# A two-layer graph kernel on one core: another order of head, step and tail, the first graph's x first on the DMA queue, fillers of other lengths

## The chip, the core and the metric

The kernel runs on one core of a Trainium2 chip. A core has five engines with a queue each: TensorE (PE, matrix products), VectorE (DVE), ScalarE (ACT), GpSimd (POOL) and SyncE (SP), which here only issues transfers. Each queue is worked off in order. An instruction that waits for another engine holds up everything behind it on its own engine. The metric is the device time of one execution in microseconds, as the median of several runs. The kernel before takes 2449.39 us (3 runs, 2448.46 to 2452.33).

## What is computed

For each of 128 graphs of 128 nodes with 512 features, in fp32:

```python
h = relu(layernorm(x))
H = (adj != 0);  w = adj[0, :]            # per graph
conv(v, W, b) = Dinv * (H @ (Binv * (H.T @ (v @ W.T)))) + b
t = relu(conv(h, W1, b1))                 # 512 -> 1024
y = conv(layernorm(t) * gamma + beta, W2, b2) + h   # 1024 -> 512
x = x + y
h = relu(layernorm(x))
agg = (adj @ h) / max(rowsum(adj), EPS)
x = x + relu(concat(h, agg) @ W.T)        # 1024 -> 512
```

`Dinv` and `Binv` are inverse weighted degrees of nodes and of hyperedges.

## The kernel before, in words

One graph is one tile: 128 nodes on the partitions, the features along the row. The weights stay in SBUF. Every large product is made with fp32 accuracy out of fp32r matrix products: each operand is split into a high part, a low part and a correction (suffixes h, l, d). `product` (L517 to L537) then issues the h and l passes into one PSUM bank (L530) and the d pass into a second (L535). Six banks carry the tag `w`, two the tag `n`. ACT makes the high part (a copy with a scale), DVE or POOL the low part, DVE the third.

A graph goes through these stages, each a small function marked `@stage`:

- `incidence...`, `node_matrix`, `node_sum`: adj is loaded in a blocked layout, transposed on DVE (L390), compared with zero (L393), its edge count and its weight scaled; PE makes the graph's 128x128 operator into `ps_s` (L430), ACT (L432) and DVE (L438) move it to SBUF as `s`.
- `x_sums`, `x_spread`, `scales`, `shifts`, `x_norm`: layer norm of x on ACT, with two tiny operations on DVE, POOL or ACT.
- `conv1_nodes` (PE, `pz`, L488), `conv1_high/low/rest` (split on ACT L501, DVE L505, L508), `conv1_weights` for two halves (PE, `rm` and `rd`), `conv1_main` (ACT L550), `conv1_out` (DVE L555), `conv1_bias` (POOL).
- `inner_...`: layer norm over 1024, then a transpose by a trip through DRAM: `inner_out` writes the tile, `inner_in` reads it in blocks by four transfers, `inner_turn` turns the blocks on DVE (L591, `nt`).
- `conv2_weights` (PE, `gm`, `gd`), `conv2_main` (ACT L690), `conv2_weights_out` (DVE L694), `conv2_bias` (POOL), `conv2_high/low/rest` and `node_high/rest` (splits), `conv2_nodes` (PE, `ym`, `yd`; at the ends of the kernel, one unsplit product `py`, L738), `conv2_out` (DVE L754).
- `layer1_...`: the layer norm of the new x, a trip through DRAM like the first (`h_scratch`, `hb`, turned into `ht`), `layer1_mean` (PE, `bm`, `bd`), `layer1_self` (PE, `am`, `ad`), `aggregate` (PE, L832), `finish` (DVE L844) and `store`.
- `mean_...`: adj divided by its row sum, turned by a third trip through DRAM (`an_scratch`, `anb`).

The order of the work is written out by hand. `head()` starts the first graphs and prepares the weights; `step(s)` for s from 3 to 124 (122 times) is the pipeline, in which the stages of seven graphs, s-4 to s+3, are interleaved; `tail()` lets the last five run out. Within a manual schedule the order of the calls is the order of each engine's queue. So a line moved in `step` moves all instructions of that stage on every engine that it uses, its transfers on SP included.

`fill(columns)` puts idle matrix products of a constant in front of the next bank's user (L100), so that PE has something to do. Tiles mostly have one buffer: `r`, `adj`, `adjb`, `ht` and the three split tiles among them. A stage that writes such a tile waits until the graph before has been read out of it.

`copy` is an ACT activation. The trace of the kernel before has one load of an activation table, 1.28 us long, and it stands ahead of `copy(eps_root, eps, AF.Sqrt)` in `head`, the first activation.

Of the kernel before, what the change touches and what calls it, by code (L numbers as in the profile page):

```python
# [24 lines left out]
def gnn_kernel(  # L25
# [760 lines left out]
    @stage  # L786
    def layer1_low(g, *eng):
        H3T[g][0](*eng)
# [67 lines left out]
    def step(s):  # L856
        node_high(s - 2)
        conv2_bias(s - 2)
        conv2_high(s - 2)
        layer1_self_main(s - 4)  # L860
        layer1_high(s - 3)
        inner_out(s - 1)
        conv2_low(s - 2, nc.vector)
        x_norm(s + 1)
        node_rest(s - 2)
        conv1_main(s, 0)
        layer1_self_out(s - 4)
        conv2_rest(s - 2)
        node_matrix(s + 1)
        conv1_weights(s, 1)  # L870
        conv1_out(s, 0)
        mean_out(s - 3)
        layer1_low(s - 3)
        layer1_rest(s - 3)
        inner_in(s - 1)
        conv2_nodes(s - 2)
        node_sum(s + 1)
        node_floor(s + 1, nc.gpsimd)
        conv2_out(s - 2)
        conv1_main(s, 1)  # L880
        conv1_out(s, 1)
        inner_turn(s - 1)
        layer1_sums(s - 2)
        mean_in(s - 3)
        layer1_spread(s - 2)
        conv1_bias(s, 0)
        load_adj(s - 2)
        incidence(s + 2)
        layer1_mean(s - 3)
        incidence_weight(s + 2, nc.vector)  # L890
        scales(s - 2, 3)
        layer1_mean_main(s - 3)
        finish(s - 4)
        conv1_bias(s, 1)
        shifts(s - 2, 3, nc.vector)
        conv1_nodes(s + 1)
        store(s - 4)
        load_x(s + 2)
        inner_high(s - 1)
        conv1_high(s + 1)  # L900
        mean_transpose(s - 3)
        layer1_mean_out(s - 3)
        layer1_self(s - 3)
        mean_operator(s - 2)
        inner_low(s - 1, nc.vector)
        inner_rest(s - 1)
        layer1_norm(s - 2)
        inner_sums(s)
        layer1_mean_high(s - 3)
        inner_spread(s)  # L910
        conv2_weights(s - 1)
        layer1_mean_low(s - 3, nc.vector)
        node_scale(s + 1)
        mean_rest(s - 3)
        layer1_trip_out(s - 2)
        x_sums(s + 2)
        incidence_count(s + 2, nc.vector)
        mean_degree(s - 2, nc.vector)
        conv2_main(s - 1)
        scales(s, 2)  # L920
        layer1_mean_rest(s - 3)
        layer1_trip_in(s - 2)
        conv1_low(s + 1)
        incidence_inverse(s + 2)
        residual(s + 1)
        mean_inverse(s - 2)
        conv2_weights_out(s - 1)
        conv1_rest(s + 1)
        shifts(s, 2, nc.gpsimd)
        load_adjb(s + 3)  # L930
        inner_norm(s)
        incidence_high(s + 2)
        layer1_turn(s - 2)
        x_spread(s + 2)
        aggregate(s - 3)
        mean_scale(s - 2, nc.vector)
        incidence_scale(s + 2, 0, nc.vector)
        scales(s + 2, 1)
        conv1_weights(s + 1, 0)
        incidence_scale(s + 2, 1, nc.vector)  # L940
        shifts(s + 2, 1, nc.vector)
        residual_bias(s + 1)
        node_up(s + 1, nc.vector)

    def head():
        load_w1(0, 0)
        load_adjb(0, nc.scalar)
        load_x(1)
        incidence(0)
        copy(eps_root, eps, AF.Sqrt)  # L950
        load_affine()
        load_x(0)
        incidence_weight(0, nc.gpsimd)
        incidence_count(0, nc.vector)
        load_w1(0, 1)
        incidence_inverse(0)
        x_sums(1, "A")
        x_sums(0)
        w1[0].high(0)
        w1[0].high(1)  # L960
        load_x(2)
        load_w1(1, 0)
        w1[0].low(0)
        incidence_high(0)
        x_spread(0)
        scales(0, 1)
        incidence_scale(0, 0, nc.gpsimd)
        incidence_scale(0, 1, nc.scalar)
        load_w1(1, 1)
        w1[0].low(1)  # L970
        w1[0].rest(1, nc.vector)
        load_adjb(1)
        shifts(0, 1, nc.gpsimd)
        x_norm(0)
        node_matrix(0)
        fill(768)
        w1[1].high(1)
        load_w2(0)
        node_sum(0)
        incidence(1)  # L980
        conv1_nodes(0)
        w1[1].high(0)
        residual(0)
        node_floor(0, nc.vector)
        incidence_count(1, nc.vector)
        load_adjb(2)
        w1[0].rest(0, nc.vector)
        x_spread(1)
        load_bias(b2_bc, b2)
        load_bias(b1_bc, b1)  # L990
        w1[1].low(1)
        incidence_inverse(1)
        conv1_high(0)
        conv1_low(0)
        conv1_rest(0)
        node_scale(0)
        incidence_weight(1, nc.gpsimd)
        conv1_weights(0, 0)
        incidence_high(1)
        w1[1].low(0)  # L1000
        incidence_scale(1, 0, nc.scalar)
        w1[1].rest(0, nc.vector)
        incidence_scale(1, 1, nc.scalar)
        load_adj(0)
        node_up(0, nc.scalar)
        conv1_main(0, 0)
        scales(1, 1)
        load_w2(1)
        node_matrix(1)
        shifts(1, 1, nc.gpsimd)  # L1010
        incidence(2)
        node_sum(1)
        incidence_count(2, nc.gpsimd)
        beta_row(0)
        conv1_out(0, 0)
        w1[1].rest(1, nc.vector)
        x_sums(2)
        beta_row(1)
        conv1_weights(0, 1)
        incidence_weight(2, nc.vector)  # L1020
        node_floor(1, nc.gpsimd)
        x_spread(2)
        scale_w2(0, nc.vector)
        scales(2, 1)
        x_norm(1)
        beta_row(2)
        load_x(3)
        shifts(2, 1, nc.gpsimd)
        incidence_inverse(2)
        conv1_bias(0, 0, nc.vector)  # L1030
        scale_w2(1, nc.scalar)
        w2[0].high(0)
        beta_row(3)
        incidence_high(2)
        conv1_nodes(1)
        load_adjb(3)
        scale_w2(2, nc.vector)
        conv1_main(0, 1)
        load_w3(1)
        mean_operator(0)  # L1040
        node_scale(1)
        scale_w2(3, nc.scalar)
        incidence_scale(2, 0, nc.vector)
        incidence_scale(2, 1, nc.scalar)
        w2[0].high(1)
        conv1_out(0, 1)
        residual_bias(0)
        conv1_high(1, True)
        node_matrix(2)
        conv1_bias(0, 1, nc.vector)  # L1050
        beta_row(4)
        beta_row(5)
        x_norm(2)
        node_sum(2)
        conv1_nodes(2)
        mean_degree(0, nc.vector)
        node_up(1, nc.gpsimd)
        node_floor(2, nc.vector)
        inner_sums(0)
        inner_spread(0)  # L1060
        residual(1)
        node_scale(2)
        residual(2)
        load_adjb(4)
        conv1_low(1)
        scale_w2(5, nc.vector)
# [3 lines left out]
        incidence_weight(3, nc.gpsimd)  # L1070
        conv1_rest(1)
        incidence_count(3, nc.gpsimd)
        scales(0, 2)
        incidence_inverse(3)
        conv1_low(2)
        beta_row(6)
        shifts(0, 2, nc.vector)
        beta_row(7)
        w2[1].high(0)
        conv1_rest(2)  # L1080
        incidence_high(3)
        w2[0].low(1)
        unit()
        scale_w2(6, nc.vector)
        inner_norm(0)
        x_sums(3)
        scale_w2(7, nc.scalar)
        w2[0].low(0)
        mean_inverse(0)
        w2[1].low(0)  # L1090
        node_up(2, nc.scalar)
        incidence_scale(3, 0, nc.vector)
        w2[1].high(1)
        conv1_weights(1, 0)
        conv1_weights(1, 1)
        incidence_scale(3, 1, nc.scalar)
        conv1_main(1, 0)
        conv1_main(1, 1)
        inner_out(0)
        w2[0].rest(0)  # L1100
        inner_in(0)
        conv1_out(1, 0)
        x_spread(3)
        w2[0].rest(1)
        conv1_out(1, 1)
        conv1_bias(1, 0, nc.vector)
        conv1_bias(1, 1, nc.vector)
        inner_sums(1)
        node_matrix(3)
        conv1_weights(2, 0)  # L1110
        scales(3, 1)
        incidence(4)
        w2[1].low(1)
        inner_spread(1)
        w2[1].rest(1, nc.gpsimd)
        incidence_weight(4, nc.vector)
        load_x(5)
        inner_turn(0)
        beta_out()
        scales(1, 2)  # L1120
        conv1_weights(2, 1)
        incidence_count(4, nc.gpsimd)
        inner_high(0)
        shifts(1, 2, nc.scalar)
        node_sum(3)
        inner_norm(1)
        w3[1].high(1)
        w3[1].high(0)
        load_x(4)
        shifts(3, 1, nc.gpsimd)  # L1130
        inner_low(0, nc.vector)
        load_w3(0)
        incidence_inverse(4)
        inner_rest(0)
        x_norm(3)
        w2[1].rest(0, nc.vector)
        incidence_high(4)
        conv2_weights(0)
        mean_scale(0, nc.scalar)
        conv1_nodes(3)  # L1140
        conv2_main(0)
# [419 lines left out]
```

## Time and profile before

| What | us |
|---|---|
| median of 3 runs | 2449.39 |
| the profiled execution | 2447.67 |
| its span, first to last instruction | 2445.9 |
| PE busy in the span | 2422.7 |
| DVE busy | 2298.1 |
| ACT busy | 2009.9 |
| POOL busy | 1324.8 |
| PE idle from 0 to 16.88, before its first product with weights | 12.34 |
| PE idle from 16.88 to 71 | 2.55 |
| PE idle from 71 to 2353 | 0.35 |
| PE idle from 2353 to the last matmul's end at 2440.73 | 2.78 |
| from there to the end | 5.17 |

The page gives busy times of each engine and its share of the span; waits are listed as "engine, line, what was waited for: total, times, longest". In the timeline each row is a start, a duration, an engine and a line. Rows that follow each other are merged ("x4"). Matmul ends are modelled, so neighbouring rows overlap; the distance between two starts is the safer measure of what an instruction costs its queue. The same holds on DVE and ACT, where the next start comes some 0.06 to 0.1 us before the printed end of the one before. The granted TensorE clock is 1.00 in every slice. The step recurs every 18.74 to 18.75 us: the product `gm` starts at 1203.46, 1222.20 and 1240.95.

### The profile page before, as it was taken

Reading aid. Unit: us, or ns where it says so; the run is one execution under the profiler, and the core shown is the slowest. Engines: PE = TensorE matmul, PEld = TensorE weight load, DVE = VectorE, ACT = ScalarE, POOL = GpSimd, SP = SyncE. Lnnn points to the kernel's source line nnn. Section 1 sums busy time; section 2 is a strip of 40 time slices with the busy share of each in tenths; the row PEclk is TensorE's granted clock in tenths of the full one; section 3 lists DMA queues with packets and bytes.
Section 4 is the critical chain, followed back from the end, with each engine's and each line's share of the span. In section 5 each row is a group of like instructions: output and inputs, shape, how many; then the busy total and the mean of one; then the engine's idle time right before and its main releaser. Section 6 shows DMA issues by size and latency. Waiting matters only on the chain.

```text
span 2445.9 us, 41647 instructions
## 1 busy us (share of the span) xinstructions
PE 2422.7 (99%) x11170; PEld 2009.6 (82%) x11170; DVE 2298.1 (94%) x5843; ACT 2009.9 (82%) x4512; POOL 1324.8 (54%) x1808
## 2 busy tenths in 40 slices
PE   7999999999999999999999999999999999999998
PEld 5788888888888888888888888888888888888886
DVE  8899999999999999999999999999999999999987
ACT  8888888888888888888888888888888888888785
POOL 5555555555555555555555555555555555555552
PEclk9999999999999999999999999999999999999999
DMA  6344433344434443444344443434343444344432
GB/s 186 114 129 125 130 124 129 124 130 128 129 119 130 132 126 123 129 129 127 124 128 128 126 129 123 132 123 130 122 133 121 130 127 131 119 131 131 127 124 92
DMA packets 408956, 311.39 MB, mean 127 GB/s; under 512 B 176656, under 2 KB 339984, under 8 KB 408720
## 3 DMA queue, kind: packets, MB, share of 16 engines
q1 hardware_dynamic: 407888, 308.66, 40.1%
q8 instruction: 88, 1.44, 0.2%
q14 instruction: 148, 1.21, 0.2%
q10 hardware_dynamic: 576, 0.07, 0.0%
q0 software_dynamic: 256, 0.01, 0.0%
HBM read 166.21 MB, written 142.34 MB: 126 GB/s over the span
## 4 chain that ended last, share of the span: by engine, by line
PE 95%; ACT 2%; DVE 1%; DMA 1%; issue 1%; SPq 0%; POOL 0%; POOLq 0%; DVEq 0%; ACTq 0%
PE gm L530 19%; PE rm L530 18%; PE am L530 9%; PE bm L530 9%; PE gd L535 9%; PE rd L535 9%; PE bd L535 5%; PE ad L535 5%; PE pz L488 4%; PE am L832 2%; PE ad L832 1%; PE ym L743 1%; PE yd L744 1%; PE ym L742 1%; PE ps_s L430 1%
## 5 line engine op out<-in xcount | busy, mean ns | idle before, releaser
L306 ACT ACTIVATE h<-x_t 128x512 f32<-128x512 f32 x255 | 159.1, 624 | 291.8 <-DVE x_t L754 283.8
L81 POOL TENSOR_TENSOR r<-r,b_bc 128x256 f32<-128x256 f32 x500 | 358.7, 739 | 70.1 <-DVE r L555 54.4
L300 POOL TENSOR_SCALAR st<-st 128x1 f32<-128x1 f32 x130 | 82.3, 633 | 569.9 <-DVE st L317 563.2
L81 POOL TENSOR_TENSOR hl<-ht,hh 128x256 fp32r<-128x256 f32 x250 | 235.4, 963 | 216.5 <-ACT hh L612 216.5
L81 POOL TENSOR_TENSOR x_t<-x_t,h 128x256 f32<-128x256 f32 x256 | 239.8, 959 | 1.3 <-ACT h L326 1.1
L81 POOL TENSOR_TENSOR g<-g,c 128x256 f32<-128x256 f32 x246 | 177.6, 743 | 72.4 <-DVE g L694 72.4
L326 ACT ACTIVATE h<-x_t,st 128x512 f32<-128x512 f32 x255 | 206.1, 808 | 2.0 <-POOL st L300 1.2
L555 DVE SCALAR_TENSOR_TENSOR r<-rd,dinv,r 128x512 f32<-128x512 f32 x256 | 190.8, 746 | 7.7 <-ACT r L550 6.3
L81 POOL TENSOR_TENSOR x_t<-x_t,b_bc 128x256 f32<-128x256 f32 x256 | 187.2, 752 | 0.0
L311 ACT ACTIVATE h<-x_t,st 128x512 f32<-128x512 f32 x255 | 182.9, 717 | 4.1
L550 ACT ACTIVATE r<-rm,dinv 128x512 f32<-128x512 f32 x256 | 174.7, 684 | 7.7 <-PE rm L530 4.4
L694 DVE SCALAR_TENSOR_TENSOR g<-gd,g 128x512 f32<-128x512 f32 x127 | 87.8, 691 | 79.5 <-issue 70.4
L621 DVE SCALAR_TENSOR_TENSOR nd<-nh,nl 128x1024 fp32r<-128x1024 f32 x127 | 155.5, 1225 | 4.2
L326 ACT ACTIVATE r<-r,st 128x1024 f32<-128x1024 f32 x128 | 157.8, 1233 | 0.1
L591 DVE STREAM_TRANSPOSE nt<-nb 128x1024 f32<-128x1024 f32 x127 | 156.9, 1235 | 0.4 <-DMA nb<-n_scratch 0.3
L81 DVE TENSOR_TENSOR nl<-nt,nh 128x1024 fp32r<-128x1024 f32 x127 | 153.5, 1208 | 1.9 <-ACT nh L612 1.7
L530 PE MATMUL am<-w31h,hh 128*128 128x512 f32 x504 | 146.8, 413 | 0.0
L311 ACT ACTIVATE junk<-r,st 128x1024 bf16<-128x1024 f32 x128 | 145.2, 1134 | 0.1
L488 PEld LDWEIGHTS pz<-s,h 128*128 128x128 f32 x1024 | 134.5, 192 | 11.1 <-ACT h L326 0.7
L530 PE MATMUL rm<-w11h,z 128*128 128x512 f32 x512 | 140.3, 396 | 0.0
L530 PE MATMUL rm<-w11l,z 128*128 128x512 f32 x512 | 139.3, 393 | 0.0
L530 PE MATMUL rm<-w10h,z 128*128 128x512 f32 x512 | 138.2, 392 | 0.9 <-ACT z L501 0.9
(244 smaller groups left out, 7594.1 us busy)
## 6 DMA issues: line engine op xcount, KB each, us to landing
n_scratch<-r SPq DMA_DIRECT2D x128, 512.0 KB, 2.6
nb<-n_scratch SPq DMA_DIRECT2D x508, 128.0 KB, 2.8
x_t<-in_x_dram SPq DMA_DIRECT2D x128, 256.0 KB, 2.7
h_scratch<-h SPq DMA_DIRECT2D x127, 256.0 KB, 2.3
hb<-h_scratch SPq DMA_DIRECT2D x508, 64.0 KB, 1.9
out_dram<-o SPq DMA_DIRECT2D x127, 256.0 KB, 2.0
adj_t<-in_adj_dram SPq DMA_DIRECT2D x128, 64.0 KB, 1.9
an_scratch<-adj_t SPq DMA_DIRECT2D x128, 64.0 KB, 1.6
```

The lines of the kernel that those rows point to most:

```text
L81: eng.tensor_tensor(dst[:, s], a[:, s], b[:, s], op)
L306: copy(junk, src, func, accum_out=t[:, 0:1])
L311: copy(junk, src, AF.Square, bias=t[:, 1:2], accum_out=t[:, 2:3])
L326: copy(dst, src, func, bias=t[:, 5:6], scale=t[:, 4:5])
L488: nc.tensor.matmul(z[:, k * P : (k + 1) * P], H0[g][:, k * P : (k + 1) * P], S[g], start=True, stop=True)
L530: nc.tensor.matmul(pm, left[i](k), right(i, k), start=(i == 0 and k == 0), stop=(i == 1 and k == kk - 1))
L535: nc.tensor.matmul(pd, left[2](k), right(2, k), start=(k == 0), stop=(k == kk - 1), skip_group_check=True)
L550: copy(R[g][:, HALVES[half]], PY.pop((g, half)), AF.Copy, scale=DN[g][:, 1:2])
L555: nc.vector.scalar_tensor_tensor(r, PR.pop((g, half)), dn[:, 0:1], r, MUL, ADD)
L591: nc.vector.transpose(nt.rearrange("p k (i b) -> p k i b", b=B), t.rearrange("p i k a -> p k i a"))
L621: nc.vector.scalar_tensor_tensor(t, h, 2.0**-12, low, MUL, SUB)
L694: nc.vector.scalar_tensor_tensor(G[g], PG.pop(g), 4096.0, G[g], MUL, ADD)
```

## The change

The set of stages stays. What changes is the order of the calls in `head`, `step` and `tail`, the engine of some tiny operations, and the fillers: 768 columns in front of the first `pz` become 1152, and 256 columns in front of the second `pz` are new. In `step`, the weight of the incidence goes from DVE to ACT. In `head`, x of graph 0 is the first transfer on SP, ahead of the first weights; a copy of weights (`w1[0].high(0)`) stands ahead of the square root of eps on ACT; x of graph 2 is issued behind the second graph's adj. No new function is called. The core of the diff:

```diff
     def step(s):
+        conv2_bias(s - 2)
+        layer1_self_main(s - 4)
+        conv1_weights(s, 1)
         node_high(s - 2)
-        conv2_bias(s - 2)
         conv2_high(s - 2)
-        layer1_self_main(s - 4)
+        mean_out(s - 3)
+        node_rest(s - 2)
         layer1_high(s - 3)
         inner_out(s - 1)
+        conv1_main(s, 0)
         conv2_low(s - 2, nc.vector)
+        layer1_low(s - 3)
+        layer1_self_out(s - 4)
+        conv1_out(s, 0)
+        node_matrix(s + 1)
+        conv2_rest(s - 2)
+        layer1_rest(s - 3)
         x_norm(s + 1)
...
+        conv1_main(s, 1)
+        conv2_nodes(s - 2)
+        layer1_mean(s - 3)
+        node_sum(s + 1)
         inner_in(s - 1)
...
+        conv2_out(s - 2)
...
+        layer1_sums(s - 2)
         conv1_out(s, 1)
+        conv1_bias(s, 0)
+        layer1_self(s - 3)
         inner_turn(s - 1)
...
+        incidence(s + 2)
+        layer1_mean_main(s - 3)
+        incidence_count(s + 2, nc.vector)
+        load_adj(s - 2)
         mean_in(s - 3)
...
-        incidence_weight(s + 2, nc.vector)
+        incidence_weight(s + 2, nc.scalar)
         scales(s - 2, 3)
-        layer1_mean_main(s - 3)
+        conv1_nodes(s + 1)
         finish(s - 4)
...
+        inner_high(s - 1)
+        inner_sums(s)
         shifts(s - 2, 3, nc.vector)
...
         store(s - 4)
+        layer1_norm(s - 2)
+        mean_transpose(s - 3)
         load_x(s + 2)
-        inner_high(s - 1)
+        inner_low(s - 1, nc.vector)
+        layer1_mean_out(s - 3)
+        layer1_mean_high(s - 3)
+        inner_rest(s - 1)
...
+        conv2_weights(s - 1)
+        load_adjb(s + 3)
+        layer1_mean_low(s - 3, nc.vector)
         conv1_high(s + 1)
...
     def head():
+        load_adjb(0, nc.scalar)
+        load_x(0)
         load_w1(0, 0)
-        load_adjb(0, nc.scalar)
+        w1[0].high(0)
         load_x(1)
         incidence(0)
+        load_w1(0, 1)
         copy(eps_root, eps, AF.Sqrt)
         load_affine()
-        load_x(0)
-        incidence_weight(0, nc.gpsimd)
-        incidence_count(0, nc.vector)
-        load_w1(0, 1)
+        x_sums(0)
...
         incidence_inverse(0)
+        w1[0].low(0)
+        x_spread(0)
         x_sums(1, "A")
-        x_sums(0)
-        w1[0].high(0)
+        incidence_high(0)
+        scales(0, 1)
         w1[0].high(1)
+        load_adjb(1)
         load_x(2)
...
         incidence_scale(0, 1, nc.scalar)
...
+        node_matrix(0)
+        w1[1].high(1)
         w1[0].low(1)
+        incidence(1)
+        fill(1152)
...
-        node_matrix(0)
-        fill(768)
...
+        conv1_main(0, 1)
+        fill(256)
+        load_bias(b2_bc, b2)
+        conv1_out(0, 1)
+        mean_operator(0)
         conv1_nodes(1)
...
     def tail():
...
+        conv2_weights_out(d)
...
+        layer1_turn(c)
+        conv2_bias(d, nc.vector)
+        mean_scale(d, nc.vector)
+        layer1_high(c)
...
-        conv2_weights_out(d)
-        conv2_bias(d, nc.vector)
-        layer1_turn(c)
-        mean_scale(d, nc.gpsimd)
...
```

The order of the built program on each engine, which shows how the change moves instructions, has one row on ACT that the text of the change does not show. Where the kernel before loads an activation table once, ahead of the square root, the changed kernel loads one ahead of `w1[0].high(0)` and another ahead of the square root:

```
1 L274 DMACopy adjb<-in_adj_dram 32x4x32 x4
2 L179 LoadActFuncSet
3 L179 Activation w10h<-w10r 128x1024
4 L953 LoadActFuncSet
5 L953 Activation eps_root<-eps 128x1
6 L306 Activation h_125,st<-x_t 128x512
```

## The prediction

> **What bounds the kernel now.** I read the page's head first, then the waits of PE, then the busy times of PE in stretches, and last the timeline of one step and of the first 20 us.
>
> ```profile
> span 2445.9 us, 41647 instructions
> PE 2422.7 (99%) x11170; PEld 2009.6 (82%) x11170; DVE 2298.1 (94%) x5843; ACT 2009.9 (82%) x4512; POOL 1324.8 (54%) x1808
> ```
>
> PE is idle for 23.2 us of the span. Its waits say where (columns: engine, line, what was waited for, total, times, longest):
>
> ```profile
> PE ps_s L430 <- ACT sb L298: 11.4, 1, 11.4
> PE py L738 <- DVE g L81: 2.1, 2, 1.1
> PE py L738 <- POOL w11ds L81: 1.7, 1, 1.7
> ```
>
> Each happens once or twice: head and tail. In stretches PE is idle 12.34 us up to 16.88, 2.55 us from there to 71, 0.35 us from 71 to 2353, 2.78 us to the last matmul and 5.17 us behind it. So the 122 steps run on PE alone, 18.74 us each. They cannot get shorter by a new order: the list of matmuls per step is the same, and a new order can only open gaps. What can be won is 2.55 + 0.35 + 2.78 = 5.7 us, plus whatever brings the first product forward. How near DVE and ACT are to the limit, from their waits between 500 and 2300 us, 96 steps:
>
> ```profile
> DVE g L694 <- issue: 57.6, 96, 0.6
> ```
>
> ```profile
> ACT h L306 <- DVE x_t L754: 230.9, 96, 2.7
> ```
>
> DVE has one gap per step, 0.6 us, ahead of L694, where it waits for `gd` on PE. ACT has a gap of 2.4 us ahead of `layer1_sums`.
>
> **The step.** I walk each queue in the new order by hand. Zero is the start of the first `rm` of `conv1_weights(s, 1)`, 1212.25 in the timeline; intervals are distances between starts in that step. PE in the new order: rm 0, rd 1.82, ps_s 2.73, ym 2.85, yd 3.33, bm 3.55, bd 5.37, am 6.28, ad 8.10, pz 9.01, gm 9.81, gd 13.52, aggregate 15.33, rm of the next half 16.01, end 18.74. ps_s moves behind `rm`, pz behind `am`; each position of gm and gd is within 0.1 us of before.
>
> DVE is fixed to PE at two points. At 15.59 L694 may start (before: aggregate's start plus 0.26). Near 3.40 L438 may start: ps_s ends at 2.85, ACT copies it (0.27, start some 0.2 later). That second wait is new. Behind it on ACT stand `x_norm` and the second `conv1_main`, which go from about 0.5 and 2.05 to 3.3 and 4.0. It costs nothing: x_norm is needed by pz at 9.01, the bank of `rm` by am at 6.28, and ACT's gap of 2.4 us was there anyway. From L694 to L438 DVE has 0.61 + 0.59 + 0.26 + 0.63 + 0.08 + 0.19 + 0.13 + 0.18 + 0.08 + 0.21 + 0.20 + 0.61 + 0.60 + 0.68 + 0.68 + 0.61 = 6.34 us of work in a room of 3.40 + 18.74 - 15.59 = 6.55. From L438 to L694 it has 11.7 us and a wait of 0.1 for ACT's L312, in a room of 12.19. The sum is what it was, less 0.07 for the weight that went to ACT. So DVE keeps 0.2 + 0.4 = 0.6 us.
>
> PE's needs: gp's correction L731 is ready at 2.6, yd wants it at 3.33. hd ends at 3.3 for bd at 5.37. On ACT, L801 starts at 7.3, the added L298 (0.15 to 0.2 us) follows, `nh` runs 7.95 to 9.0 for gm at 9.81 (before 8.7 for 9.79). nl ends at 10.3 for 11.7, nd at 12.1 for 13.5, bl and bd at 13.1 and 14.4 for 15.5, the split of z at 12.2, 15.1 and, a round later, 16.9 for 16.0, 16.9 and 17.8. All in time: cost 0.
>
> SP: four `adjb` issues of 0.46 us now stand ahead of `h_scratch`, and on ACT L306/L307 of `inner_sums` (1.18 us) ahead of the `layer1_norm` that feeds it. `layer1_norm` ends at 11.0 (before 10.1); store at 8.7, x at 9.1 and adjb at 9.55 to 11.4 let `h_scratch` go at 11.45 (before 10.12). It lands 2.3 later, four `hb` issues take 1.3 to the last one, which lands 1.9 later: 17.0. DVE comes to `ht` at 17.05 (before: 15.85 for 16.94). The cover shrinks from 1.1 us to 0.05, with DVE's 0.6 behind it. `n_scratch` goes at 16.15 (before 16.4), behind hb and `an_scratch`; the four nb land at about 5.2 for `nt` at 5.7, as before. `adj_t` and `anb` follow and land by 7.5, for 8.5 and 8.8.
>
> A rule speaks against this: the Trainium skill, SBUF — State Buffer (SBUF: two separate sides), says that a DVE operation with two SBUF inputs and a POOL operation that reads SBUF take one port pair in turn, each for a whole instruction. The trace agrees in one place per step:
>
> ```profile
> 1219.43 1.90 POOL L81 TENSOR_TENSOR x_t<-x_t,h 128x256 f32<-128x256 f32 x2
> ...
> 1219.68 1.04 DVE L844 SCALAR_TENSOR_TENSOR o<-o,x_t 128x512 f32<-128x512 f32 x1
> ```
>
> L844 takes 0.65 in the tail and 1.04 here. In the new order POOL's `hl` meets gp and L731, and its x_t meets nl. By bare durations that is 0; by the rule 0.2 + 0.15. I take 0 for PE, since both ends stay below DVE's 0.6.
>
> **The head.** ACT loads a second table, between `w10h(0)` and eps_root. The row:
>
> ```profile
> 2.69 1.28 ACT L950 ACT_TABLE_LOAD   x1 [2.69 <-issue]
> 3.99 0.20 ACT L950 ACTIVATE eps_root<-eps 128x1 f32<-128x1 f32 x1
> ...
> 10.85 0.40 ACT L298 ACTIVATE sb<-adjt,sb 128x128 fp32r<-128x128 f32 x1
> ```
>
> The new first load lies under the transfers. Then `w10h(0)` waits for 256 + 512 KB; before, that many bytes (first weights, then x of graph 1) had landed at 5.74. So 5.75 + 1.04, table 1.28, eps 0.2: x_sums(0) starts at 8.2 (before 6.60); x landing first buys nothing, as ACT comes to it late. Then 0.86 + 1.04 + 0.86 + 0.1 + 0.95 + 0.55 to ps_s(0): 12.6 (before 11.40), +1.2. By the page ScalarE: Activation LUTs (What ACT_TABLE_LOAD costs) a switch takes 2.66 us, with a drain of 1.38. The row shows 1.28 and eps_root 0.02 behind it, but on an engine that had nothing to drain. I take the row; the page would add 1.4.
>
> The filler of 768 columns took from 11.75 to 14.31, 3.33 ns each; 1152 take 3.84 and end at about 16.8. x_norm(0) is ready at 12.05 + 0.35 + 1.04 + 0.95 + 0.25 + 0.95 + 0.81 = 16.4, so the filler costs 0.4 and the rest is ACT's order. pz starts at 16.8, +2.5 against 14.31; it takes 1.63 slow or 0.85 fast (51.62 shows the fast one), and `rm` follows by 16.88's distance: 18.6 to 19.4 against 16.88. Say +2.2. The filler of 256 columns adds 0.43 us at the fast rate, or 0 if PE waits for s there anyway. Back come some of the head's 2.55 us: `rm` of graph 3 now stands between gd(1) and the `wd` products, which saves waits of 0.39 and 0.2; but `conv1_out(2,0)` (0.66) goes ahead of `conv2_bias(0)`, for which py waits. DMA: x of graph 2 goes from 4.6 to about 10.5; ACT wants it near 20. Sum +2.2 + 0.3 - 0.5 = +2. Ends: 0, if later waits soak up the late start, and +4 with the drain and cold products.
>
> **The tail.** PE's last five rounds have the same order but for pz and ps_s. py still stands behind the bias of graphs d and e. `layer1_turn(c)` (0.7) goes ahead of `conv2_bias(d)`: py +0.7, the bm behind it -0.65. Sum 0, ends -2 (most of the 2.78) and +2.
>
> **The sum.** Execution 2447.67 + 0 (steps) + 2 (head) + 0 (tail) = 2449.7. The median stood 1.7 above this execution: 2451.4.
>
> **The rivals.** (1) The h trip and DVE become the loop of the step, slower. If hb lands later than about 17.6 (0.6 behind my 17.0), or port waits add up to more than DVE's 0.6, the excess is paid in each step: 0.1 us is 12.2 us. For it: cover of 0.05 at ht, DVE at 97%, hb landings up to 3.0 in the trace. Against: medians of 1.9, and two cushions. A likely excess of 0.05 to 0.2 gives 2457 to 2476. (2) Head and tail get better: the start is soaked up and half of the tail's waits go: 2446 to 2448; more than 4.9 below would need nearly all of the 5.7 us and no late start. (3) The change does nothing: same steps, and the head's late start absorbed: 2449.4; it lies inside the first range.
>
> **How the numbers follow.** Likeliest case with (3), 2447.5 to 2454.5: 0.60. Rival (1): 0.32. Rival (2): 0.08. 0.2% is 4.9 us, about what a measurement can tell from no change. Faster by more: 0.04 out of (2). Slower: all but a little of (1), and the top of the first case: 0.33. Same: 0.63. The range runs from 2447 to 2472: it leaves out half of (2) and the upper third of (1).
>
> **What would show it.** Right: PE idle from 71 to 2353 under 2 us, gm every 18.74, ps_s(0) near 12.6, pz(0) near 16.8, two table loads. Wrong: a wait of `bm`, `yd` or `nh` repeated 122 times (rival 1), DVE waiting for hb, the first `rm` at or before 17, or a PE step other than 18.74.

## The result and the profile after

The changed kernel takes 2463.27 us (median of 5, 2461.16 to 2463.65) against 2449.39 (5 runs, 2448.46 to 2452.33): ratio 1.0052, 95% interval 1.0038 to 1.0067, so 13.9 us slower. The profiled execution took 2463.27, its span 2461.5.

The head of the page, first the span, then the busy times. PE has the same products as before but for the fillers, DVE is 3.9 us less busy, ACT 18.5 us more:

```profile
span 2461.5 us, 41531 instructions
...
PE 2427.9 (99%) x11174; PEld 2007.9 (82%) x11174; DVE 2294.2 (93%) x5732; ACT 2028.4 (82%) x4632; POOL 1306.7 (53%) x1797
```

PE's waits (total, times, longest). The first line is the head, 0.7 us more than before. The next two are new, and they lie in the steps: `yd` waits for its operands, but in 16 of 118 steps, not in each. (The releaser is inferred. `yd` does not read the `h` of L326; in all 16 it starts 0.15 us behind the end of L731.)

```profile
PE ps_s L430 <- ACT sb L298: 12.1, 1, 12.1
PE yd L744 <- DVE sp L731: 4.7, 10, 0.9
PE yd L744 <- ACT h L326: 3.6, 6, 0.6
PE py L738 <- DVE g L81: 2.8, 2, 1.5
PE py L738 <- POOL w11ds L81: 1.7, 1, 1.7
PE pz L488 <- ACT h L326: 1.2, 1, 1.2
```

DVE's waits between 500 and 2300 us. Before, its one large wait was L694, 57.6 us in 96 steps. That has shrunk to 15.2, and a wait for hb, here as it was before, leads the list:

```profile
DVE ht L591 <- DMA hb<-h_scratch: 0.5, 1, 0.5
```

After:

```profile
DVE ht L591 <- DMA hb<-h_scratch: 20.1, 29, 1.5
...
DVE g L694 <- issue: 15.2, 54, 0.3
DVE s L438 <- ACT s L432: 8.6, 35, 0.3
DVE ht L591 <- PE rm L530: 5.1, 5, 1.1
```

The five waits put down to `rm` are for hb too: ht starts 0.12 or 0.18 us behind hb's landing in them, as in the others. ACT's gap ahead of `layer1_sums` (230.9 us before) is split in two, as ps_s now comes later:

```profile
ACT s L432 <- PE ps_s L430: 180.8, 96, 2.2
ACT h L306 <- DVE x_t L754: 82.6, 95, 1.9
```

To place the loss I cut each profiled execution at three marks on PE: the first `rm`, the first and the last `yd` of the steps. "Long" are the intervals from yd to yd over 18.95 us; a usual interval is 18.75, and the sum is what the long ones exceed the usual one by. The marks are of one execution each, and the executions of the kernel before alone lie between 2446.82 and 2453.05 us, so a difference of 1 or 2 us between two rows is weak.

```
                  median   first rm  first yd  yd..yd    last yd..last matmul  long: n, sum
before            2449.39  16.88     108.58    2194.92   137.23                 5,  1.5
after             2463.27  18.38     109.53    2208.20   138.24                21, 12.3
step_alone        2461.05  16.68     108.57    2208.32   136.96                20, 12.1
head_alone        2453.86  18.45     110.04    2198.45   137.60                11,  4.2
tail_alone        2450.98  16.56     108.33    2194.79   139.74                 2,  0.8
adjb_back         2553.75  18.86     110.69    2298.47   137.68               115, 105.1
h_first           2543.12  18.63     110.73    2289.18   137.51               117,  95.8
adjb_early        2457.60  18.69     109.55    2202.04   138.18                13,  6.5
early_norm        2460.51  17.89     109.73    2205.61   138.54                18, 10.3
turn_late         2453.26  18.78     109.77    2197.25   137.08                 4,  1.8
adjb_between      2452.31  17.81     109.55    2199.04   138.58                 9,  4.3
before_adjb       2475.95  17.09     108.88    2223.79   136.98                41, 30.0
mended            2449.73  16.73     107.73    2199.36   136.56                 8,  3.7
mended_old_ends   2448.78  16.49     109.89    2195.52   137.48                 1,  0.7
```

Of the changed kernel's 15.2 us between the two last matmuls (2440.73 and 2455.97), 0.95 is in the head, 13.3 in the steps and 1.0 in the tail. Against usual steps the loss there is 14.8 us, and it was 1.5 before: 12.3 lie in 21 long steps, 2.5 in 32 that are 0.03 to 0.2 us longer, mostly those behind a long one, in which DVE, now nearly without gaps, works off its delay. (The two waits of yd listed sum to 8.3 us, not to 13.3: the 16 intervals are 0.69 us longer in the mean, with a listed wait of 0.52, and the waits in the other five long ones are too short to be listed.)

**One late step.** Rows of SP's queue in one step and, behind the dots, in the next:

```profile
1191.21 1.88 SPq L274 DMA_DIRECT2D adjb<-in_adj_dram  x4
1193.19 0.38 SPq L576 DMA_DIRECT2D h_scratch<-h  x1
1195.26 1.73 SPq L584 DMA_DIRECT2D hb<-h_scratch  x4
...
1211.94 0.38 SPq L576 DMA_DIRECT2D h_scratch<-h  x1
1215.52 1.73 SPq L584 DMA_DIRECT2D hb<-h_scratch  x4
```

From `h_scratch` to `hb` SP waits for the landing: 2.07 us in the first step, 3.58 in the second. What this does to DVE and, a step boundary later, to PE:

```profile
1218.87 0.71 DVE L591 STREAM_TRANSPOSE ht<-hb 128x512 f32<-128x512 f32 x1 [1.16 <-DMA hb<-h_scratch]
```

```profile
1223.19 0.47 PE L744 MATMUL yd<-sp 128*128 128x512 f32 x1 [0.52 <-DVE sp L731]
```

ht is 1.16 us late. DVE's own 0.6 takes up half, and L731, the eleventh operation behind ht, is 0.52 late for yd. It is the same in all 16: DVE takes 4.18 us from the start of ht to the end of L731, which is the median of the other steps too, and yd starts 4.32 to 4.33 us behind ht. So nothing between ht and yd is slower, and the delay comes in with hb. The DMA view of the late trip, 1211.9 to 1215.5, shows what else was moved; in the step before, 1193.1 to 1195.3, there was only q1, which carries the kernel's own transfers:

```profile
q8 instruction: 1, 0.02, 2.5%
q14 instruction: 1, 0.01, 0.6%
...
h_scratch<-h SPq DMA_DIRECT2D x1, 256.0 KB, 3.5
```

q8, of the kind "instruction", carries 89 packets in the execution, 1.46 MB, so 16.4 KB each. I counted them for every step between the issue of x and ht: all 16 steps in which yd waits have one; of the 102 others, 15 have one. With them the trip is late at one of three places: the landing of h_scratch (3.1 to 3.6 us instead of 2.1, in 6 of the 16), the landing of hb (6), or SP's own issues (4; four adjb took 3.39 us instead of 1.88 at 1021). The kernel before has them too: in seven of its steps hb was issued 3.3 to 3.5 us behind h_scratch instead of 2.5, each with a q8 packet, and yd never waited.

### The profile page after: what moved, and what is told of

Same layout as the page of the kernel before. It is cut to its first block, busy times and chain, and to the rows that moved or that the text cites. A ratio compares the mean times of both kernels' runs of the same rounds, so it can differ in the third digit from the quotient of the medians.

```text
span 2461.5 us, 41531 instructions
## 1 busy us (share of the span) xinstructions
PE 2427.9 (99%) x11174; PEld 2007.9 (82%) x11174; DVE 2294.2 (93%) x5732; ACT 2028.4 (82%) x4632; POOL 1306.7 (53%) x1797
## 3 DMA queue, kind: packets, MB, share of 16 engines
q8 instruction: 89, 1.46, 0.3%
## 4 chain that ended last, share of the span: by engine, by line
PE 86%; ACT 5%; DVE 4%; DMA 2%; issue 1%; SPq 1%; POOL 0%; DVEq 0%; ACTq 0%
PE rm L530 17%; PE gm L530 16%; PE bm L530 8%; PE am L530 8%; PE rd L535 8%; PE gd L535 8%; PE pz L488 4%; PE bd L535 4%; PE ad L535 4%; PE am L832 2%; PE yd L744 1%; DMA hb<-h_scratch 1%; PE ad L832 1%; PE ym L743 1%; PE ym L742 1%
## 5 line engine op out<-in xcount | busy, mean ns | idle before, releaser
L81 POOL TENSOR_TENSOR hl<-ht,hh 128x256 fp32r<-128x256 f32 x242 | 216.5, 914 | 169.0 <-ACT hh L612 169.0
L432 ACT ACTIVATE s<-ps_s 128x129 f32<-128x129 f32 x128 | 35.8, 279 | 227.5 <-PE ps_s L430 227.5
L326 ACT ACTIVATE h<-x_t,st 128x512 f32<-128x512 f32 x255 | 205.0, 804 | 2.0 <-DVE st L300 2.0
L555 DVE SCALAR_TENSOR_TENSOR r<-rd,dinv,r 128x512 f32<-128x512 f32 x256 | 189.7, 741 | 2.6 <-ACT r L550 1.9
L550 ACT ACTIVATE r<-rm,dinv 128x512 f32<-128x512 f32 x256 | 173.8, 680 | 16.1 <-DMA n_scratch<-r 10.9
L326 ACT ACTIVATE r<-r,st 128x1024 f32<-128x1024 f32 x128 | 157.9, 1234 | 0.8 <-DVE st L300 0.8
L530 PE MATMUL gm<-w20h,nh 128*128 128x512 f32 x508 | 147.7, 412 | 0.0
L530 PE MATMUL bm<-w30h,hh 128*128 128x512 f32 x504 | 138.0, 396 | 0.0
```

The source lines that it names most:

```text
L81: eng.tensor_tensor(dst[:, s], a[:, s], b[:, s], op)
L326: copy(dst, src, func, bias=t[:, 5:6], scale=t[:, 4:5])
L530: nc.tensor.matmul(pm, left[i](k), right(i, k), start=(i == 0 and k == 0), stop=(i == 1 and k == kk - 1))
L550: copy(R[g][:, HALVES[half]], PY.pop((g, half)), AF.Copy, scale=DN[g][:, 1:2])
L555: nc.vector.scalar_tensor_tensor(r, PR.pop((g, half)), dn[:, 0:1], r, MUL, ADD)
```

## The experiments

Theory: the cover of the h trip (the time by which hb lands ahead of its use) is gone, so DVE waits for hb in the steps in which the trip is late, and yd stands behind it. Rivals: the new place of ps_s and x_norm, or a shared port, delays yd; or head and tail carry the loss. Each run below has its own comparison with the kernel before (2448.59, 2449.70 and 2449.42 us in the three groups).

**step_alone**: head and tail of before, `step` of after.

> The kernel before with the new step alone; head and tail as before. Theory (the h trip comes late in some steps, DVE waits for hb, and yd behind it): the steps carry nearly all of the loss, 2449.4 + 13.3 = 2462.7 us, with a wait of yd for L731 or L326 in about 16 of 118 steps. Rival (head and tail carry it: second table load, the first product 1.5 us later): within 1 us of 2449.4.

2461.05 us, ratio 1.0048 (1.0035 to 1.0060): +12.5, and 13.4 us more from yd to yd, with 18 waits of yd. The loss is in the step. (19 of its 20 long steps have a q8 packet.)

**head_alone**: `head` of after, the rest of before.

> The kernel before with the new head alone. Theory: the head carries 1 us of the loss (yd of the first steady step comes at 109.5 where it came at 108.6): 2450.4 us, first rm near 18.4, no wait of yd in the steps. Rival (head and tail): +5 us or more.

2453.86 us, ratio 1.0020 (1.0013 to 1.0027): +5.3, which neither side had. Only 1.5 us of it lie ahead of the first yd. 3.5 lie in the steps, whose order is that of before: 11 long ones instead of 5. PE's waits for it are short, and they are for DVE:

```profile
PE ps_s L430 <- DVE st L300: 0.7, 3, 0.4
```

The parts are not additive (12.5 + 5.3 + 1.3 is more than 13.9): with the new step, the new head adds nothing between the yd marks (2208.20 and 2208.32).

**adjb_back**: undo one move of the change.

```diff
-        load_adjb(s + 3)          # ahead of layer1_mean_low(s - 3)
...
         conv1_rest(s + 1)
+        load_adjb(s + 3)
```

> The changed kernel with load_adjb(s + 3) moved back behind conv1_rest(s + 1), so that h_scratch no longer stands behind four adjb issues on SP. Theory: h_scratch goes when layer1_norm ends, 11.05 us after the first rm instead of 11.48; each stall of yd shrinks by up to 0.43, and those below that vanish: some 5 us of 13 stay, 2455.5 us (2453 to 2458). Rival (ps_s and x_norm behind the first rm, or a shared port, set the stalls): 2463, unchanged.

2553.75 us, ratio 1.0432 (1.0418 to 1.0447). Both sides missed by 90 us and more. ACT's waits between 500 and 2300 us name what I had overlooked:

```profile
ACT r L550 <- DMA n_scratch<-r: 122.9, 86, 2.3
```

Behind adjb on SP stands `n_scratch`. It now goes 18.65 us after the first rm of `conv1_weights(s, 1)` in the median (16.31 in the changed kernel), and the tile r that it reads has one buffer. `conv1_main(s, 0)`, which the change moved near the front of the step, writes that tile. So the early conv1_main needs an early n_scratch, and moving adjb away from there was part of the same bargain; adjb_between, below, tests this.

**h_first**: as adjb_back, and `inner_sums(s)` moved behind `layer1_norm(s - 2)`.

> The changed kernel with load_adjb(s + 3) moved back behind conv1_rest(s + 1) and inner_sums(s) moved behind layer1_norm(s - 2): SP and ACT both let h_scratch go first. Theory: h_scratch goes about 9.8 us after the first rm (11.48 in the changed kernel, 10.12 before), hb lands 1.7 us earlier, ahead of nearly every ht; 0 to 1.6 us of the 13.3 stay, and head and tail keep their 2: 2450 to 2453 us. Rival (ps_s and x_norm behind the first rm, or a shared port): 2463, unchanged.

2543.12 us, ratio 1.0380 (1.0365 to 1.0394): the same wall, L550 waits for n_scratch 80.1 us in 56 steps. So it does not test the h trip.

**adjb_early**: adjb where SP was idle.

```diff
         mean_in(s - 3)
+        load_adjb(s + 3)
...
-        load_adjb(s + 3)
```

> The changed kernel with load_adjb(s + 3) moved forward behind mean_in(s - 3), into SP's idle stretch ahead of the store, instead of ahead of h_scratch. Putting it behind hb cost 90 us, because n_scratch then went 1.9 us later and r, which has one buffer, waited for it. Here nothing is put between hb and n_scratch. Theory (h trip late, cover 0.05): h_scratch goes 11.05 us after the first rm instead of 11.48 and is never held by adjb; of the 13.3 us lost in the steps some 4 stay: 2454 us (2451 to 2457), with at most 6 waits of yd. Rival (ps_s and x_norm behind the first rm, or a shared port): 2463, unchanged.

2457.60 us, ratio 1.0032 (1.0020 to 1.0043): about half of the step's loss is back, on the theory's side but above its upper bound by a little. adjb, with one buffer, waits for L393 and pushes store and x up to h_scratch. h_scratch goes at 10.93 (11.48 in the changed kernel), but SP goes on to hb 2.29 us later in the median instead of 2.09, and over 3 us later in 23 steps instead of 7.

**early_norm**: adjb_early, and `inner_sums(s)` behind `layer1_norm(s - 2)`.

> The changed kernel with load_adjb(s + 3) moved forward behind mean_in(s - 3) and inner_sums(s) moved behind layer1_norm(s - 2). Theory: h_scratch goes about 9.9 us after the first rm (before: 10.12), the cover of hb is 1.1 us or more again, and nearly all of the 13.3 us come back; head and tail keep some 2: 2450 to 2452 us. If the later inner_sums makes n_scratch late, ACT's L550 waits for it and the time is above that of adjb_early. Rival (ps_s and x_norm behind the first rm, or a shared port): 2463.

2460.51 us, ratio 1.0045 (1.0032 to 1.0057): a miss. h_scratch goes at 10.00, as I wanted, but its trip takes 3.30 in the median, and over 3 us in all but one of the steps. It went 1.48 us earlier than in the changed kernel and was there 0.27 earlier. The load of x, 256 KB issued 0.53 us before it, is still on the way. It is so in the other runs too (x lands 2.7 to 3.1 us behind its issue); what differs is the distance. Medians, in us; "its trip" is the time until SP issues hb:

```
               h_scratch behind x   its trip   sum
early_norm     0.53                 3.30       3.83
h_first        0.77                 3.17       3.94
before         1.24                 2.52       3.76
adjb_early     1.46                 2.28       3.72
adjb_between   1.90                 2.04       3.95
after          2.46                 2.09       4.55
```

Up to a distance of 1.9 the sum stays between 3.72 and 3.95: an issue closer to that of x did not bring hb's issue forward. That x's bytes hold the store up would fit; no run takes x away.

**turn_late**: the transfers stay, the one who waits for them comes later.

```diff
-        layer1_turn(s - 2)        # behind x_spread(s + 2)
...
         node_up(s + 1, nc.vector)
+        layer1_turn(s - 2)
```

> The changed kernel with layer1_turn(s - 2) alone moved, to the end of the step behind node_up(s + 1): five short DVE operations, 0.63 us, go ahead of ht. SP and ACT keep their order and the transfers go when they did. Theory: the cover of hb grows from 0.05 to 0.7; what is left of the single stalls (0.3 to 0.9 us each) is about 2 us, so 2452 us (2451 to 2455), and DVE's waits for hb fall from 29 to a few. Rival (the cost is a shared port or the place of ps_s, and hb only shows it): 2463.

2453.26 us, ratio 1.0015 (1.0008 to 1.0021): 10 of the 13.9 us are back with no transfer moved. PE's waits in the steps, all of them:

```profile
PE yd L744 <- DVE sp L731: 1.0, 2, 0.8
```

Between 500 and 2300 us DVE's waits for hb are gone from its list; one wait of 1.1 us at ht is left. The edit leaves the place of ps_s and of x_norm as it is, so these do not cause the stalls. It does move five DVE operations against POOL's; that no port is behind it rests on the 4.18 us above, which are the same in stalled and other steps.

**tail_alone**: `tail` of after, the rest of before.

> The kernel before with the new tail alone. By the distance from the last yd of the steps to the last matmul (137.23 us before, 138.24 in the changed kernel) the tail costs 1 us: 2449.6 against 2448.6. If the losses of head and steps overlap and the tail gives something back, it is 1 to 3 us below the kernel before.

2450.98 us, ratio 1.0007 (1.0001 to 1.0014): +1.3. The tail costs 1 to 2.5 us by the marks (138.24 and 139.74 against 137.23).

**adjb_between**: adjb goes while SP waits for n_scratch anyway.

```diff
         inner_out(s - 1)
+        if s > 3:
+            load_adjb(s + 2)
...
-        load_adjb(s + 3)
+        if s == N - 4:
+            load_adjb(s + 3)
```

> The changed kernel with the adjb of the next graph issued between n_scratch and nb, that is load_adjb(s + 2) behind inner_out(s - 1), and not ahead of h_scratch. Putting it between hb and n_scratch cost 90 us. If that cost was n_scratch going 1.9 us later, with L550 waiting for the one buffer of r, it vanishes here, since SP waits 2.6 us for n_scratch to land at this point anyway: L550's waits for n_scratch fall from 123 us to under 10, and with h_scratch at 11.05 the time is that of adjb_early or a little less, 2455 us (2452 to 2458). If the cost was something else about taking adjb away from ahead of h_scratch, it stays above 2500.

2452.31 us, ratio 1.0014 (1.0007 to 1.0020). h_scratch goes at 10.93, its trip takes 2.04, n_scratch goes at 16.06, and ACT's wait between 500 and 2300 us is:

```profile
ACT r L550 <- DMA n_scratch<-r: 6.0, 17, 0.9
```

So the 90 us of adjb_back were n_scratch, and hb's landing 0.7 us earlier saves two thirds of the step's loss (13.3 to 4.1).

**before_adjb**: one move of the change in the kernel before.

```diff
+        load_adjb(s + 3)
         layer1_trip_out(s - 2)
...
-        load_adjb(s + 3)          # behind shifts(s, 2)
```

> The kernel before with one edit of the change alone: load_adjb(s + 3) ahead of layer1_trip_out(s - 2). SP then issues four adjb between x and h_scratch, which goes at about 11.2 us after the first rm instead of 10.12; hb lands 1.1 us later, and its cover of 1.1 is gone. Theory: this edit is most of the loss, 2449 + 8 to 13 = 2457 to 2462 us, with DVE waiting for hb in the steps in which an instruction packet delays the trip. Rival (the cover alone costs little; it takes the new order of DVE, ACT and PE as well): 2449 to 2452.

2475.95 us, ratio 1.0106 (1.0092 to 1.0120): +26.5, twice what I expected and twice the whole change. h_scratch goes at 11.37. The wait on PE is another:

```profile
PE ps_s L430 <- DVE st L300: 19.8, 32, 1.6
```

The rows of one such step, DVE, then PE:

```profile
1243.76 0.71 DVE L591 STREAM_TRANSPOSE ht<-hb 128x512 f32<-128x512 f32 x1 [0.78 <-DMA hb<-h_scratch]
1244.40 0.25 DVE L300 TENSOR_SCALAR adj_t<-adj_t,deg 128x128 f32<-128x128 f32 x1
1244.56 0.28 DVE L300 TENSOR_SCALAR sb<-adjt,sb 128x128 fp32r<-128x128 f32 x1
1244.83 0.27 DVE L300 TENSOR_SCALAR sb<-adjt,sb 128x128 fp32r<-128x128 f32 x1
...
1245.25 0.36 PE L430 MATMUL ps_s<-sb,adjt 128*128 128x258 f32 x1 [0.49 <-DVE st L300]
```

In the old order ps_s stands ahead of `rm`, and the sb that it needs comes one operation behind ht on DVE, so a late hb reaches PE with little in between. In the new order ps_s stands 2.7 us behind the step's first rm, and the need that comes first is yd's, at 3.3. With h_scratch at nearly the same place (11.37 and 11.48), the new order loses 12.3 us in long steps and the old one 30.0: the rest of the change softens what this one move costs. Only 24 of the 41 long steps have a q8 packet between x and ht, so here a loss came without one too.

**mended**: adjb_between, turn_late and, in the head, one move.

```diff
+        copy(eps_root, eps, AF.Sqrt)
         w1[0].high(0)
...
-        copy(eps_root, eps, AF.Sqrt)
```

> The changed kernel with three mends: adjb issued between n_scratch and nb, layer1_turn(s - 2) at the end of the step, and in the head eps_root ahead of w1[0].high(0), so that one table load is left. Theory: both covers are there (h_scratch 0.43 earlier, ht 0.63 later), the steps take what they took before, 2195 to 2196 us from the first to the last yd; the first rm comes 1.3 us earlier than 18.4, near 17.1. Time 2463.3 - 12.5 - 1.3 = 2449.5 us (2448 to 2452). If the steps keep 2 us or more of excess, it is not the h trip alone.

2449.73 us, ratio 1.0000 (0.9992 to 1.0008). The head gained more than said: the first rm is at 16.73 instead of 18.38, earlier than before the change. The steps missed: 2199.36 us, 8 long ones, 6 waits of yd for L731. By the mark I had set, something beside the cover of hb is left, and the trace names it: in five of the six, n_scratch lands 3.6 to 4.8 us behind its issue instead of 2.6, with a q8 packet at most 0.13 us from the issue. L550 waits 0.55 to 0.80 us for that landing, L555 on DVE then waits, and yd waits for L731; at ht DVE waits in only one of the five. The rows of another one:

```profile
2173.36 0.69 ACT L550 ACTIVATE r<-rm,dinv 128x512 f32<-128x512 f32 x1 [0.80 <-DMA n_scratch<-r]
...
2174.08 0.75 DVE L555 SCALAR_TENSOR_TENSOR r<-rd,dinv,r 128x512 f32<-128x512 f32 x1 [0.61 <-ACT r L550]
...
2175.49 0.51 PE L744 MATMUL yd<-sp 128*128 128x512 f32 x1 [0.42 <-DVE sp L731]
```

So with hb covered, the next transfer without cover is n_scratch.

**mended_old_ends**: that step between the head and the tail of before.

> The new step with the first two mends (adjb between n_scratch and nb, layer1_turn at the end of the step), between the head and the tail of the kernel before. Theory: the steps at 2195 us, head and tail as before: 2448.5 us, within 1.5 us of the kernel before. A gain of more than 2 us has nothing to come from: the kernel before loses only 1.5 us in its steps.

2448.78 us, ratio 0.9996 (0.9987 to 1.0004): no different from the kernel before, as expected. The steps take 2195.52 us. No version here beats the kernel before by what these runs can tell.

## Why the prediction was wrong in its likeliest case

The time lies inside the range given (2447 to 2472), but on the side of rival (1) and not of the likeliest case, and PE is idle for 8.7 us from 71 to 2353, where under 2 was to show that the likeliest case was right.

**The step.** Cost 0 was wrong; it is 13.3 us. The step that failed is the sentence "The cover shrinks from 1.1 us to 0.05, with DVE's 0.6 behind it", taken as no cost. Its numbers held: h_scratch at 11.48 (I said 11.45), n_scratch at 16.31 (16.15), ht at 17.31 in the median (17.05). In the median step PE does run 18.75 us, and DVE's 0.6 does absorb a small delay: of its 34 waits at ht between 500 and 2300 us, PE felt 14. But I compared one step's landing with one step's need. A transfer's duration has a tail, and the trace of before showed it: trips of 3.3 to 3.5 us seven times, and "hb landings up to 3.0", which I wrote down under a rival. A trip that is 1.1 to 1.5 us late needs a cover of that size; before, 1.1 + 0.6 was there, after, 0.05 + 0.6. The sum to make was, over all trips, the lateness beyond the cover. From the trace of before it gives some 5 us: from the issue of h_scratch to the last landing of hb, 16 of its 118 trips took over 0.65 us more than the median, and what lies beyond the 0.65 sums to 4.8 us. So the sum would have ruled out a cost of 0 and come to a third of what was measured (4.8 of 13.3). In the changed kernel DVE waited 0.95 to 1.52 us at ht in the 16 stalled steps, and these are 11 us longer (16 x 0.69); five shorter stalls and the steps in which DVE catches up bring it to the 14.8.

**Rival (1)** named the place (h trip, hb, DVE), and it came true, but not in its form. It let the excess be paid "in each step"; it was paid in 21 of 117 intervals, at 0.2 to 1.2 us each. That the time falls among its 2457 to 2476 is luck: its 0.05 to 0.2 us times 122 steps and the few large stalls happen to give the same sum.

**The need that I did not list.** n_scratch must land before `conv1_main(s, 0)` writes r again. The change moves that operation from 1.2 to 0.2 us behind the step's first rm, and I did not ask which transfer still reads its tile. In the changed kernel it fits barely (waits of L550: 5.2 us in 20 steps between 500 and 2300 us); adjb_back shows the price when it doesn't, and mended's last stalls are the same wait.

**The port rule.** I took 0 for POOL's `hl` meeting gp and L731. gp beside hl takes 0.68 (0.69 before, with no POOL operation beside it), L731 0.68 (0.73 before), and L844 became shorter, 917 ns in the mean against 1020, before and after:

```profile
L844 DVE SCALAR_TENSOR_TENSOR o<-o,x_t 128x512 f32<-128x512 f32 x118 | 120.4, 1020 | 0.0
```

```profile
L844 DVE SCALAR_TENSOR_TENSOR o<-o,x_t 128x512 f32<-128x512 f32 x118 | 108.2, 917 | 0.0
```

The bare durations were right, and no wait points to a port. The 0.35 that I had put beside them by the Trainium skill, SBUF — State Buffer (SBUF: two separate sides), did not come. L844, which in the rows shown overlaps POOL's x_t, still takes longer than the 0.64 to 0.75 in the tail, so the rule fits that pair and not gp or L731 beside hl; what sets them apart, no run here shows.

**The head.** ps_s(0) at 12.11 (12.6 said), pz(0) at 16.33 (16.8), first rm at 18.38 (18.6 to 19.4), and +0.95 at the first yd where I had +2. The rows of ACT:

```profile
5.29 1.06 ACT L179 ACTIVATE w10h<-w10r 128x1024 fp32r<-128x1024 f32 x1 [1.37 <-DMA w10r<-in_w1t_dram]
6.36 1.28 ACT L953 ACT_TABLE_LOAD   x1
7.66 0.20 ACT L953 ACTIVATE eps_root<-eps 128x1 f32<-128x1 f32 x1
...
11.67 0.39 ACT L298 ACTIVATE sb<-adjt,sb 128x128 fp32r<-128x128 f32 x1
```

The second table load starts 0.01 us behind the end of `w10h(0)` and costs 1.28, with 0.02 behind it. The 1.38 us for a drain of the Trainium skill, ScalarE: Activation LUTs (What ACT_TABLE_LOAD costs), do not show, on an engine that this time had just worked; the row was the right choice. mended shows the price of the order: with the square root first, x_sums(0) starts at 6.29 instead of 7.77, which is the load and eps_root, and the first rm comes 1.65 us earlier (the other runs with the new head have it at 17.81 to 18.86). What I missed is that the head changes the steps: the old step behind the new head takes 2198.45 us instead of 2194.92. The new head ends at another moment, with another number of instructions ahead, so the late trips fall on other steps (a q8 packet between x and ht in 30 of 118 steps instead of 22, and in 8 of the 11 long ones); that would do it, but no run here changes only that, and it stays open.

**The tail.** 0 +- 2 was said; it is +1.0 to +2.5 by the marks and +1.3 (0.2 to 3.4) by the medians.

**What is not settled.** That q8 packets make the trips late rests on their coincidence, 16 of 16 against 15 of 102; no run took packets away, and some long steps have none (2 of 21 in the changed kernel, 5 of 18 in early_norm, 17 of 41 in before_adjb). The Trainium skill, Runtime: NRT & Kernel Launch (Instruction fetch mechanics), says that an engine's instruction memory is refilled in blocks of 16 KiB by its own DMA queue while it runs on, at a cost that is "mostly hidden". The 16.4 KB per packet agree. What these traces add is that a data transfer beside such a packet came 1.1 to 1.5 us late. If the packet is the cause, its cost is hidden only as long as that transfer has cover.

## What to carry to other kernels

Cover for a transfer is measured against its slow landings, not its median: count how often it is late in the whole trace, by how much, and what then waits. When a stage moves forward in a queue, list the transfers that still read the tile it writes, above all where the tile has one buffer. And when an order is tight, two edits paid: letting the waiting instruction come later (turn_late, 10 us), and taking other issues out of the way of the transfer (adjb_between, 11 us). Pushing the transfer close behind another large one did not (early_norm, 3 us).

## What the hardware showed that was not expected

- A 256 KB store issued 0.53 us behind the 256 KB load of x took 3.30 us in the median, one issued 1.90 behind it 2.04: it was there 3.8 to 3.9 us behind the issue of x in both.
- A 16.4 KB instruction packet and a late transfer coincide in all 16 steps in which yd waits; in 4 of them it is SP that takes 3.1 to 3.5 us for four issues that usually take 1.88.
- A table load between two busy stretches of ACT took 1.28 us, with 0.01 us ahead of it and 0.02 behind.
